# Moving the query and key projections of a pipelined self-attention ahead by one slot, placing the softmax sums between two parts of a step, and giving the last inverses a second DMA queue

## The chip, the cores and the metric

The kernel runs on one core of one Trainium2 chip. The metric is the device time of one execution in microseconds (us). Engines are named as in the profile: PE is TensorE (its weight loads are shown as PEld), DVE is VectorE, ACT is ScalarE, POOL is GpSimd, SP is SyncE, which issues the DMAs. Each engine works through its own instructions in order; what ties the engines together are waits on semaphores.

## The reference, cut to what matters

Two transformer blocks run one after the other on x of shape 8 x 512 x 256, all in float32. The first (L0) has an adaptive layer norm, self-attention with 16 heads of 16, cross-attention and a gated feed-forward. The second (L1), around which everything here turns, begins with self-attention of 16 heads of 64:

```python
q = _heads(xq @ wq)
k, v = jnp.split(ctx @ wkv, 2, axis=-1)      # here ctx is xq
q = _rope(q, sq, cq)
k = _rope(k, sk, ck)
sim = jnp.einsum('bhnd,bhmd->bhnm', q, k) * DH ** (-0.5)
a = jax.nn.softmax(sim, axis=-1)
o = jnp.einsum('bhnm,bhmd->bhnd', a, v)
o = o.transpose(0, 2, 1, 3).reshape(xq.shape[0], xq.shape[1], MID)
return o @ wo + bo
```

It is followed by a cross-attention over 64 context rows and a feed-forward with gelu.

## The kernel before, in words

The program has stages: the whole of L0 (about 24 to 880 us in the profile), the self-attention of L1 (880 to about 2057 us with its tail), the cross-attention of L1 (to about 2425 us), the feed-forward of L1 (to the end). The diff touches only the second of these, the block under the pool named "ph4". In it the order of the instructions on PE, DVE, ACT and POOL is the order in which the Python code issues them (a manual schedule over these four engines). SP is not part of it, nor are the stages that follow: their instructions are ordered by the framework's scheduler, which can also put instructions of a later stage between those of this one.

**The loop.** For each of 8 batches (`batch4`), the 16 heads are cut into 4 groups `g` of 4 heads, and the 512 keys into 4 tiles `kt`. One step `i` of the loop in `slots` stands for one pair (g, kt), 16 steps to a batch, 128 in all. Step `i` issues first `score` of its own pair, then `value` of the pair of step `i - 1`, and after every odd step the list `steps[i // 2]`, called a slot here. A group thus has four steps and two slots; slot `base + 2 * g` (with `base = 8 * b`) closes steps kt = 0 and 1 of group g, slot `base + 2 * g + 1` closes kt = 2 and 3.

- `score` (8 calls of `mm`, each two matmul instructions in the profile[...]; tile ps_S, four heads side by side) is followed by two exponentials on ACT (line 892, tile p).
- `value` has 4 calls of `mm` into the banks ps_O and ps_D, which are held for the four steps of a group. At kt = 0 POOL adds p of tile 0 and p of tile 1 (line 907, tile sm, twice); at kt = 2 DVE adds p of tiles 2 and 3 to it (line 911, four times); at kt = 3 ACT copies the two banks to oT (line 915).
- `queries(g)` and `keys(g)` both call `turned`: 4 calls of `mm` (8 instructions) into two ps_X banks, four products with the rotary tables on DVE (lines 871 and 872, tile t), a difference and a sum on POOL (lines 874 and 875, tile q or k). All matmuls have line 107, that of the helper `mm`; they are told apart by their tiles.
- `sums(g)` adds sm over the partitions with matmuls against ones, ACT copies the result (line 923, tile den), and it goes through DRAM to the layout 128 x 16: den_d is written (line 925), rec is read (line 927).
- `inverse(g)` takes the reciprocal on DVE (line 931), writes it to DRAM (line 933) and reads it back spread over the partitions, two tiles rb (line 937). `scaled(g)` multiplies the two oT of the group with them (line 942, POOL).
- `out_tiles` projects oT of all groups with w_so and adds it to x (line 396); `values` projects v (copies on line 861); `rows_` is the layer norm of the next batch (DVE statistics on lines 187, 188 and 178, POOL power on line 179, DVE result z on line 191), `turn` transposes it to hT (line 366, copies on line 367).

**Where they stand before the change.** queries(g) is in slot base + 2g - 2 and keys(g) in slot base + 2g - 1; the latter is the slot just before score(g, 0). sums(g) and inverse(g) are in slot base + 2g + 2, scaled(g) in the slot after that. The next batch's rows_, turn, queries(0) and keys(0) are in slots base - 4, base - 2, base - 2 and base - 1.

**Buffers.** ps_X has two banks, ps_S two tiles, ps_O and ps_D one each. q0, q1, k0, k1, v have two buffers, t four, p six, sm four, rb three, hT one.

**The tail.** After the last step come the values of the cross-attention to follow, `cross_values(p)` for p = 0 to 7 (2 calls of `mm`, a copy on ACT on line 830 into the two buffers named k0, and a store v_d on line 831). sums(3), inverse(3) and scaled(3) of the last batch stand before p = 2, 5 and 6. Then the last `out_tiles` follow. All these DMAs are issued by SP.

Of the kernel before, what the change touches and what calls it, by code (L numbers as in the profile page):

```python
# [17 lines left out]
B, N, D, H, T, CD, FF = 8, 512, 256, 16, 64, 192, 1024  # L18
# [60 lines left out]
def fast_path(ctx: ExitStack, tc: tile.TileContext, a: dict, out: bass.AP):  # L79

    nc = tc.nc
# [8 lines left out]
    def bank_s():  # L90
        return psum.tile([P, 2, 512], F32, tag="S", name="ps_S", bufs=2)
# [7 lines left out]
    def bank_x():  # L99
        if turns:  # L100
            turns[0] += 1
            if turns[0] % 3 == 0:
                return bank_d()
        return psum.tile([P, 512], F32, tag="X", name="ps_X", bufs=2)

    def mm(o, lhsT, rhs, start=True, stop=True):
        nc.tensor.matmul(o, lhsT, rhs, start=start, stop=stop)  # L107
# [38 lines left out]
    def check(src):  # L146
        c = checks[0]
        checks[0] += 1
        for i, op in enumerate((ALU.max, ALU.min)):
            nc.vector.tensor_reduce(chk[:, i, c : c + 1], src, AX.X, op)  # L150
# [258 lines left out]
    def flat(d):  # L409

        v = d.rearrange({2: "h n -> (h n)", 3: "j e n -> (j e n)"}[len(d.shape)])
        return v.rearrange("(p i) -> p i", p=P)
# [393 lines left out]
    def kv_first():  # L806
        w = wpool.tile([P, 2, NPAIR, 2, T], F32, tag="w4", name="kv", bufs=1)
        kvs.append((w[:, 0], w[:, 1]))
        return kvs[0]
# [6 lines left out]
    def load_vb(b):  # L816
        for e in range(2):
            r = slice(64 * e, 64 * e + 64)
            nc.sync.dma_start(kvs[b % 2][1][r, :, e, :], v_d[b, r])
# [5 lines left out]
    def cross_values(wk, p):  # L825
        ps = bank_x()
        for k in range(2):
            mm(ps, cross["v"][:, k, p * P : (p + 1) * P], ctxzT[:, k, :], k == 0, k == 1)
        v = wk.tile([P, N], F32, tag="k0", name="v")
        nc.scalar.copy(v, ps)  # L830
        nc.sync.dma_start(v_d[:, :, p, :].rearrange("b r t -> r b t"), v.rearrange("p (b t) -> p b t", b=B))


    with tc.tile_pool(name="ph4", bufs=2) as wk:
        NG = H // 4
        kb, vb = kv_first()
        steps = {}

        def last(slot, fn):
            steps.setdefault(slot, []).append(fn)  # L840

        def batch4(b):
            s = {}
            base = 2 * NG * b
# [8 lines left out]
            def values(half, ts):  # L853
                if ts[0] == 0:
                    s["v", half] = wk.tile([P, NT, 512], F32, tag="v", name="v")
                for t in ts:
                    ps = bank_x()
                    for k in range(2):
                        mm(ps, s["hT"][:, k, t * P : (t + 1) * P], w_sv[:, k, half * 512 : (half + 1) * 512],
                           k == 0, k == 1)  # L860
                    nc.scalar.copy(s["v", half][:, t, :], ps)

            def turned(g, w, tag, pss=None):

                even, odd = pss or (bank_x(), bank_x())
                for e, ps in enumerate((even, odd)):
                    for k in range(2):
                        mm(ps, w[:, k, (2 * g + e) * P : (2 * g + e + 1) * P], s["hT"][:, k, :], k == 0, k == 1)
                ec, es, oc, os = (wk.tile([P, N], F32, tag="t", name="t", bufs=4) for _ in range(4))
                for ps, c, sn in ((even, ec, es), (odd, oc, os)):  # L870
                    nc.vector.tensor_tensor(c, ps, rope_c, ALU.mult)  # L871
                    nc.vector.tensor_tensor(sn, ps, rope_s, ALU.mult)  # L872
                s[tag, g] = r = [wk.tile([P, N], F32, tag=f"{tag}{e}", name=f"{tag}{e}") for e in range(2)]
                nc.gpsimd.tensor_tensor(r[0], ec, os, ALU.subtract)  # L874
                nc.gpsimd.tensor_tensor(r[1], es, oc, ALU.add)  # L875

            def queries(g, pss=None):
                turned(g, w_sq, "q", pss)

            def keys(g, pss=None):  # L880
                turned(g, w_sk, "k", pss)
# [12 lines left out]
            def value(g, kt):  # L894
# [17 lines left out]
                if kt == NT - 1:  # L912
                    for u in range(2):
                        s["oT", 2 * g + u] = o = wk.tile([P, N], F32, tag="oT", name="oT", bufs=10)
                        nc.scalar.copy(o, s["o", u])

            def sums(g):

                d = bank_x()
                for j in range(4):  # L920
                    mm(d[32 * j : 32 * j + 32, :], ones32, s["sm", g, j // 2][:, j % 2, :])
                den = wk.tile([P, N], F32, tag="den", name="den", bufs=1)
                nc.scalar.copy(den, d)
                s["dd", g] = dd = dram.tile([4, N], F32, tag="den_d", name="den_d")
                nc.sync.dma_start(dd, den.rearrange("(j r) n -> j r n", j=4)[:, 0, :])
                s["rec", g] = rec = wk.tile([P, 4 * N // P], F32, tag="rec", name="rec")
                nc.sync.dma_start(rec, flat(dd))

            def inverse(g):
                rec = s["rec", g]  # L930
                nc.vector.reciprocal(rec, rec)
                s["inv", g] = d = dram.tile([4, N], F32, tag="rec_d", name="rec_d")
                nc.sync.dma_start(flat(d), rec)
                check(rec)
                for u in range(2):
                    s["rb", g, u] = rb = wk.tile([P, N], F32, tag="rb", name="rb", bufs=3)
                    nc.sync.dma_start(rb, d[2 * u : 2 * u + 2, None, :].to_broadcast([2, 64, N]))

            def scaled(g, engines=None):
                for u, eng in enumerate(engines or [nc.gpsimd] * 2):  # L940
# [4 lines left out]
                project_out(qp, lambda k: s["oT", k], w_so, 8, add_to(b))  # L945

            if b:
                last(base - 4, rows_)
                last(base - 2, turn)
                last(base - 2, lambda: values(0, (0, 1)))  # L950
                last(base - 2, lambda: queries(0))
                last(base - 1, lambda: values(0, (2, 3)))
                last(base - 1, lambda: keys(0))
            else:
                s["hT"] = ready

                def begin():
                    queries(0)
                    both = bank_s()
                    keys(0, (both[:, 0, :], both[:, 1, :]))  # L960
                    values(0, (0, 1))
                    values(0, (2, 3))

                last(-1, begin)
                last(4, lambda: [nc.gpsimd.memset(z, 0.0) for z in (kb, vb)])
                last(5, lambda: load_kb(0))
            for h in range(2):
                last(base + h, lambda h=h: values(1, (2 * h, 2 * h + 1)))
            for g in range(1, NG):
                last(base + 2 * g - 2, lambda g=g: queries(g))  # L970
                last(base + 2 * g - 1, lambda g=g: keys(g))
            return score, value, sums, inverse, scaled, out_tiles

        todo = [batch4(b) for b in range(B)]
        for b, (score, value, sums, inverse, scaled, out_tiles) in enumerate(todo):
            base = 2 * NG * b
            for g in range(NG):
                if b == B - 1 and g == NG - 1:
                    break
                n = base + 2 * g + 2  # L980
                steps.setdefault(n, []).insert(0, lambda g=g, f=sums: f(g))
                last(n, lambda g=g, f=inverse: f(g))
                last(n + 1, lambda g=g, f=scaled: f(g))
            if b < B - 1:
                for qp in range(2):
                    steps[base + 2 * NG + 2 + qp].insert(0, lambda qp=qp, f=out_tiles: f(qp))

        def slots():
            n = B * NG * NT
            for i in range(-2, n + 1):  # L990
                if 0 <= i < n:
                    todo[i // 16][0](i % 16 // NT, i % NT)
                if 1 <= i <= n:
                    todo[(i - 1) // 16][1]((i - 1) % 16 // NT, (i - 1) % NT)
                if i % 2:
                    for fn in steps.get(i // 2, []):
                        fn()
                if i == n - 5:
                    cross_weights()
            sums, inverse, scaled, out_tiles = todo[-1][2:6]  # L1000
            for p in range(NPAIR):
                if p == 2:
                    sums(NG - 1)
                if p == 5:
                    inverse(NG - 1)
                if p == 6:
                    scaled(NG - 1, [nc.gpsimd, nc.vector])
                cross_values(wk, p)
            load_vb(0)
            for qp in range(2):  # L1010
                out_tiles(qp)

        with tc.manual_schedule(engines={ENG.PE, ENG.DVE, ENG.Activation, ENG.Pool}):
            slots()
# [94 lines left out]
    with tc.tile_pool(name="ph6", bufs=2) as wk:  # L1109
# [22 lines left out]
        for b in range(B):  # L1132
            hT = ready
            hid = wk.tile([P, 8, N], F32, tag="hid", name="hid")
            for ff in range(4):
                ps = bank_s()
                for i in range(2):
                    f = 2 * ff + i
# [874 lines left out]
```

## Time and profile before

The time before is 2676.88 us, the median of three runs (2672.62 to 2684.0). The profiled execution has a span of 2670.4 us.

| what | us |
|---|---|
| PE busy | 2477.0 (93% of the span) |
| PE weight loads, beside the matmuls | 1170.0 |
| DVE busy | 1083.8 |
| ACT busy | 874.5 |
| POOL busy | 839.6 |
| 880 to 2015 us (self-attention of L1): PE busy of 1135.0 | 1012.84 |
| the same: DVE, ACT, POOL busy | 411.12, 347.75, 417.65 |
| one steady batch of it, 1283.73 to 1427.04: PE busy of 143.31 | 128.33 |
| 2055 to 2425 us (cross-attention of L1): PE busy of 370.0 | 347.50 |
| 2425 to 2670 us (feed-forward of L1): PE busy of 245.0 | 238.58 |

A busy time is the union of an engine's instructions. In a timeline each row gives the start, the length, the engine, the line, the operation with its tile written and tiles read, and in brackets the idle time of the engine ahead of it with the one that ended it. In the table of waits each row reads: who waited, for whom, the total in us, how often, the longest.

### The profile page before, as it was taken

How to read it: one execution, taken by the hardware profiler on the slowest of the kernel's cores; microseconds unless marked ns; L12 is line 12 of the kernel's file. 1: busy time of each engine (PE TensorE's matmuls, PEld its weight loads, DVE VectorE, ACT ScalarE, POOL GpSimd, SP SyncE). 2: the span in 40 equal slices, each digit the busy share in tenths (PEclk: the TensorE clock that was granted, in tenths of full speed). 3: DMA queues.
4: the chain of work that ended last, by engine and by line, in shares of the span. 5: the costliest groups of instructions: out<-in, count | busy, mean ns of one | idle time of the engine just before them, and what ended most of it. 6: DMA issues, size and time to landing. Idle time of an engine off the chain costs nothing.

```text
span 2670.4 us, 27976 instructions
## 1 busy us (share of the span) xinstructions
PE 2477.0 (93%) x10938; PEld 1170.0 (44%) x10938; DVE 1083.8 (41%) x2039; ACT 874.5 (33%) x1099; POOL 839.6 (31%) x521
## 2 busy tenths in 40 slices
PE   8999999999999989898998989897998999999999
PEld 3333444444355433334343434343344465556665
DVE  5554444543444243434333343334332765662100
ACT  3565554554621233232323232332321211111221
POOL 3452232233010243333333332434331534331100
PEclk9999999999999999999999999998998999999999
DMA  5120000000010000000000000000113113211000
GB/s 170 37 89 10 11 19 10 12 19 10 8 61 26 1 21 17 17 17 13 17 13 17 17 17 17 17 13 13 33 49 92 48 40 80 59 45 41 16 16 25
DMA packets 91084, 83.76 MB, mean 31 GB/s; under 512 B 51104, under 2 KB 67424, under 8 KB 90936
## 3 DMA queue, kind: packets, MB, share of 16 engines
q1 hardware_dynamic: 90944, 81.89, 10.4%
q8 instruction: 88, 1.44, 0.2%
q14 instruction: 52, 0.43, 0.1%
HBM read 72.09 MB, written 9.77 MB: 31 GB/s over the span
## 4 chain that ended last, share of the span: by engine, by line
PE 81%; DVE 8%; POOL 5%; issue 3%; DMA 2%; ACT 2%; SPq 0%; DVEq 0%; POOLq 0%; ACTq 0%
PE ps_X L107 39%; PE ps_S L107 21%; PE ps_D L107 10%; PE ps_O L107 9%; POOL k L874 1%; DVE sm L911 1%; DVE t L871 1%; POOL k L875 1%; DVE t L723 1%; DVE t L872 1%; PE ps_X L366 1%; DMA rb<-rec 1%; ACT p L505 1%; DVE st L187 1%; POOL q L724 1%
## 5 line engine op out<-in xcount | busy, mean ns | idle before, releaser
L107 PE MATMUL ps_S<-q,k 32*128 32x512 f32 (+1 forms) x3072 | 459.4, 651 | 126.5 <-POOL k L874 117.8
L892 ACT ACTIVATE p<-ps_S 128x1024 f32<-128x1024 f32 x256 | 248.1, 1021 | 649.2 <-PE ps_S L107 649.2
L107 PEld LDWEIGHTS ps_S<-q,k 32*128 32x128 f32 (+1 forms) x3072 | 173.8, 190 | 373.9 <-POOL k L874 143.5
L505 ACT ACTIVATE p<-ps_S 128x1024 f32<-128x1024 f32 x256 | 248.2, 1021 | 260.1 <-PE ps_S L107 259.1
L871 DVE TENSOR_TENSOR t<-ps_X,rope_c 128x512 f32<-128x512 f32 x126 | 86.9, 690 | 468.0 <-PE ps_X L107 468.0
L911 DVE TENSOR_TENSOR sm<-sm,p 128x1024 f32<-128x1024 f32 x128 | 184.0, 1481 | 44.8 <-ACT p L892 44.8
L907 POOL TENSOR_TENSOR sm<-p 128x1024 f32<-128x1024 f32 x64 | 149.4, 2353 | 132.3 <-ACT p L892 132.3
L396 DVE TENSOR_TENSOR x<-ps_X,x 128x512 f32<-128x512 f32 x48 | 33.2, 691 | 367.3 <-PE ps_X L107 367.3
L107 PE MATMUL ps_X<-hT,w 128*128 128x512 f32 x344 | 160.6, 601 | 1.6 <-DVE t L678 1.1
L874 POOL TENSOR_TENSOR k<-t 128x512 f32<-128x512 f32 x32 | 40.4, 1261 | 363.2 <-DVE t L872 363.2
L724 POOL TENSOR_TENSOR q<-t,t 128x512 f32<-128x512 f32 x72 | 97.3, 1354 | 157.3 <-DVE t L723 149.8
L107 PE MATMUL ps_O<-p,v 128*64 128x512 f32 x512 | 144.5, 644 | 0.0
L107 PE MATMUL ps_O<-p,h 128*32 128x512 f32 x1024 | 138.1, 612 | 0.5 <-ACT oT L518 0.5
L107 PE MATMUL ps_D<-p,v 128*64 128x512 f32 x512 | 132.7, 597 | 0.0
L107 PE MATMUL ps_X<-vw,p 128*128 128x256 f32 x512 | 120.5, 392 | 9.7 <-DVE p L1090 9.6
L179 POOL TENSOR_TENSOR rstd<-rstd,mhalf 128x4 f32<-128x4 f32 x49 | 50.7, 1035 | 244.6 <-DVE rstd L178 242.5
L107 PE MATMUL ps_X<-w_sa_wo,oT 128*128 128x256 f32 x512 | 117.9, 389 | 7.8 <-POOL oT L942 4.3
L107 PE MATMUL ps_X<-w_sa_wv,hT 128*128 128x512 f32 x256 | 118.0, 604 | 0.6
L107 PE MATMUL ps_S<-hT,w_ff_w 128*128 128x512 f32 x256 | 117.9, 604 | 0.1
L107 PE MATMUL ps_X<-hT,w_ca_wq 128*128 128x512 f32 x256 | 117.3, 598 | 0.7 <-DVE t L723 0.7
L380 POOL TENSOR_TENSOR x<-x,rows 128x1024 f32<-128x1024 f32 x24 | 56.4, 2351 | 194.2 <-DVE z L191 194.2
L107 PE MATMUL ps_X<-hT,w_sa_wq 128*128 128x512 f32 x256 | 116.0, 596 | 0.0
(219 smaller groups left out, 3539.3 us busy)
## 6 DMA issues: line engine op xcount, KB each, us to landing
rb<-rec SPq DMA_DIRECT2D x80, 256.0 KB
rb<-rec_d SPq DMA_DIRECT2D x64, 256.0 KB
x<-in_x_dram SPq DMA_DIRECT2D x8, 512.0 KB
out_dram<-x SPq DMA_DIRECT2D x8, 512.0 KB
bc<-modd SPq DMA_DIRECT2D x8, 384.0 KB
gate<-modd SPq DMA_DIRECT2D x16, 128.0 KB
k_d<-q SPq DMA_DIRECT2D x8, 256.0 KB
v_d<-v SPq DMA_DIRECT2D x8, 256.0 KB
```

What stands on the lines that cost most here:

```text
L107: nc.tensor.matmul(o, lhsT, rhs, start=start, stop=stop)
L179: nc.gpsimd.tensor_tensor(r[:, :n], r[:, :n], mhalf[:, :n], ALU.pow)
L187: nc.vector.bn_stats(st[:, t, :], src[:, t, :])
L380: nc.gpsimd.tensor_tensor(xs[b], xs[b], r[:, None, :].to_broadcast([P, NT, D]), ALU.add)
L396: nc.vector.tensor_tensor(x, ps, x, ALU.add)
L505: nc.scalar.activation(pr[u], pss[u], AF.Exp, scale=HD0 ** -0.5)
L724: nc.gpsimd.tensor_tensor(dst, t1, t2, ALU.add)
L871: nc.vector.tensor_tensor(c, ps, rope_c, ALU.mult)
L874: nc.gpsimd.tensor_tensor(r[0], ec, os, ALU.subtract)
L892: nc.scalar.activation(pr, pss[u], AF.Exp, scale=HD1 ** -0.5)
L907: nc.gpsimd.tensor_tensor(sm, s["p", g, 0, u], s["p", g, 1, u], ALU.add)
L911: nc.vector.tensor_tensor(s["sm", g, u], s["sm", g, u], s["p", g, t, u], ALU.add)
```

## The change

Three things are changed, all in the self-attention of L1 and its tail.

1. **One slot earlier.** queries(g) moves to slot base + 2g - 3, keys(g) to base + 2g - 2, and with them the next batch's rows_ (base - 5), turn and queries(0) (base - 3) and keys(0) (base - 2). values(0) stays in slots base - 2 and base - 1. The purpose is that a whole slot lies between the projection of keys and the first score that reads them.
2. **Sums between values and scores.** sums(g) no longer stands in the slot after step 4g + 5 of the batch's steps, but directly after `value` of the even step before it (dictionary `mid`), the step in which the last value product of group g is issued.
3. **The tail.** sums(3) of the last batch follows the last value product at once, before the first cross_values. Its DMAs, those of its inverse included, are issued by ACT instead of SP. They are split in two calls each (`sums_back`, `inverse_back`), placed after p = 1, 3 and 5, and scaled(3) comes after the last cross_values.

```diff
+            def queue(g):
+                return nc.scalar if (b, g) == (B - 1, NG - 1) else nc.sync
...
-                nc.sync.dma_start(dd, den.rearrange("(j r) n -> j r n", j=4)[:, 0, :])
+                queue(g).dma_start(dd, den.rearrange("(j r) n -> j r n", j=4)[:, 0, :])
...
             if b:
-                last(base - 4, rows_)
-                last(base - 2, turn)
+                last(base - 5, rows_)
+                last(base - 3, turn)
+                last(base - 3, lambda: queries(0))
                 last(base - 2, lambda: values(0, (0, 1)))
-                last(base - 2, lambda: queries(0))
+                last(base - 2, lambda: keys(0))
                 last(base - 1, lambda: values(0, (2, 3)))
-                last(base - 1, lambda: keys(0))
...
             for g in range(1, NG):
-                last(base + 2 * g - 2, lambda g=g: queries(g))
-                last(base + 2 * g - 1, lambda g=g: keys(g))
+                last(base + 2 * g - 3, lambda g=g: queries(g))
+                last(base + 2 * g - 2, lambda g=g: keys(g))
...
-                steps.setdefault(n, []).insert(0, lambda g=g, f=sums: f(g))
+                mid[n] = lambda g=g, f=sums: f(g)
...
+                if i % 2 == 0 and i // 2 in mid:
+                    mid[i // 2]()
                 if i % 2:
                     for fn in steps.get(i // 2, []):
                         fn()
...
+            sums(NG - 1)
             for p in range(NPAIR):
-                if p == 2:
-                    sums(NG - 1)
-                if p == 5:
-                    inverse(NG - 1)
-                if p == 6:
-                    scaled(NG - 1, [nc.gpsimd, nc.vector])
                 cross_values(wk, p)
+                if p % 2:
+                    (sums_back, inverse, inverse_back, lambda g: None)[p // 2](NG - 1)
+            scaled(NG - 1, [nc.gpsimd, nc.vector])
```

More of the change, by code (lines that the diff above doesn't have):

```diff
@@ L836, in fast_path @@
         kb, vb = kv_first()
-        steps = {}
+        steps, mid = {}, {}
         def last(slot, fn):
@@ L924, in sums, with sums_back @@
                 s["dd", g] = dd = dram.tile([4, N], F32, tag="den_d", name="den_d")
-                nc.sync.dma_start(dd, den.rearrange("(j r) n -> j r n", j=4)[:, 0, :])
+                queue(g).dma_start(dd, den.rearrange("(j r) n -> j r n", j=4)[:, 0, :])
+                if (b, g) != (B - 1, NG - 1):
+                    sums_back(g)
+            def sums_back(g):
                 s["rec", g] = rec = wk.tile([P, 4 * N // P], F32, tag="rec", name="rec")
-                nc.sync.dma_start(rec, flat(dd))
+                queue(g).dma_start(rec, flat(s["dd", g]))
             def inverse(g):
@@ L932, in inverse, with inverse_back @@
                 s["inv", g] = d = dram.tile([4, N], F32, tag="rec_d", name="rec_d")
-                nc.sync.dma_start(flat(d), rec)
+                queue(g).dma_start(flat(d), rec)
                 check(rec)
+                if (b, g) != (B - 1, NG - 1):
+                    inverse_back(g)
+            def inverse_back(g):
+                d = s["inv", g]
                 for u in range(2):
                     s["rb", g, u] = rb = wk.tile([P, N], F32, tag="rb", name="rb", bufs=3)
-                    nc.sync.dma_start(rb, d[2 * u : 2 * u + 2, None, :].to_broadcast([2, 64, N]))
+                    queue(g).dma_start(rb, d[2 * u : 2 * u + 2, None, :].to_broadcast([2, 64, N]))
             def scaled(g, engines=None):
@@ L969, in batch4 @@
             for g in range(1, NG):
-                last(base + 2 * g - 2, lambda g=g: queries(g))
-                last(base + 2 * g - 1, lambda g=g: keys(g))
-            return score, value, sums, inverse, scaled, out_tiles
+                last(base + 2 * g - 3, lambda g=g: queries(g))
+                last(base + 2 * g - 2, lambda g=g: keys(g))
+            tail = sums, sums_back, inverse, inverse_back, scaled, out_tiles
+            return score, value, sums, inverse, scaled, out_tiles, tail
         todo = [batch4(b) for b in range(B)]
-        for b, (score, value, sums, inverse, scaled, out_tiles) in enumerate(todo):
+        for b, (score, value, sums, inverse, scaled, out_tiles, _) in enumerate(todo):
             base = 2 * NG * b
@@ L999, in slots @@
                     cross_weights()
-            sums, inverse, scaled, out_tiles = todo[-1][2:6]
+            sums, sums_back, inverse, inverse_back, scaled, out_tiles = todo[-1][-1]
+            sums(NG - 1)
             for p in range(NPAIR):
-                if p == 2:
-                    sums(NG - 1)
-                if p == 5:
-                    inverse(NG - 1)
-                if p == 6:
-                    scaled(NG - 1, [nc.gpsimd, nc.vector])
                 cross_values(wk, p)
+                if p % 2:
+                    (sums_back, inverse, inverse_back, lambda g: None)[p // 2](NG - 1)
+            scaled(NG - 1, [nc.gpsimd, nc.vector])
             load_vb(0)
```

## The prediction

> **What bounds the kernel now.** I read the page first: its busy times, and the chain that ended last.
>
> ```profile
> span 2670.4 us, 27976 instructions
> ...
> PE 2477.0 (93%) x10938; PEld 1170.0 (44%) x10938; DVE 1083.8 (41%) x2039; ACT 874.5 (33%) x1099; POOL 839.6 (31%) x521
> ...
> PE 81%; DVE 8%; POOL 5%; issue 3%; DMA 2%; ACT 2%; SPq 0%; DVEq 0%; POOLq 0%; ACTq 0%
> ```
>
> PE is the bound, and 2670.4 - 2477.0 = 193 us of the span have no matmul. The second view is the table of waits in the stage that changes (885 to 2060 us), the rows in which PE waits or which concern the spread inverses:
>
> ```profile
> PE ps_S L107 <- POOL k L874: 117.8, 31, 13.4
> ...
> POOL oT L942 <- DMA rb<-rec_d: 42.1, 10, 16.1
> ```
>
> 31 times, once for each group but the first, the scores wait for POOL to finish the keys. That is most of the idle time of PE in the kernel. The third view is PE's timeline in one steady batch (1283.73 to 1427.04, 143.31 us): first an ordinary stall, then the one that occurs once a batch.
>
> ```profile
> 1302.14 3.60 PE L107 MATMUL ps_X<-hT,w_sa_wk 128*128 128x512 f32 x8
> 1308.60 2.36 PE L107 MATMUL ps_S<-q,k 32*128 32x512 f32 x16 [2.86 <-POOL k L874]
> ...
> 1404.38 3.70 PE L107 MATMUL ps_X<-hT,w_sa_wk 128*128 128x512 f32 x8
> 1414.04 3.80 PE L107 MATMUL ps_S<-q,k 32*128 32x512 f32 x16 [5.96 <-POOL k L874]
> 1417.77 1.98 PE L107 MATMUL ps_O<-p,v 128*64 128x512 f32 x4
> ...
> 1420.68 2.00 PE L107 MATMUL ps_S<-q,k 32*128 32x512 f32 x16
> ```
>
> The ordinary stall is pure latency: keys' matmuls, two DVE products, POOL's difference, then the scores, with nothing in between to do. The longer one comes where the next batch's layer norm holds DVE up. After it the matmuls also run slower: score plus value take 1420.68 - 1414.04 = 6.64 us, against 3.80 us elsewhere (below). The fourth view is the chain of waits in the tail:
>
> ```profile
> 2012.64 7.60 DMA v_d<-v
> ...
> 2020.98 6.93 PE ps_X L107 x8
> ...
> 2029.63 12.48 DMA rb<-rec_d
> ...
> 2042.96 13.53 PE ps_X L107 x50
> ```
>
> After the last value product (ends at 2010.0) the last projection waits for spread inverses that are issued at 2029.05 and take 12.48 us.
>
> [...]after 2.86 us of idling the scores take 2.36 us, after 5.96 us 3.80.[...]
>
> **The change part by part.**
>
> Keys a slot earlier: no operation is added, the same 8 matmuls, 4 products and 2 POOL operations move. Removed are the 31 waits, 117.8 us. For half-speed matmuls after the longer waits: the eight long ones (seven near 6, one of 13.39 us) cost 6.64 - 3.80 = 2.8 us more, 22.4 us. The 21 ordinary ones cost 4.16 - 3.80 = 0.36 us (1308.60 to 1312.76; the second half of the scores waits for POOL's second operation), 7.6 us. The two in the first batch cost 1.64 and 1.44 us. Sum 33.
>
> Is the new distance long enough? A step without extra work takes 3.80 us (1290.80 to 1294.60). After keys' last matmul the order is now step 4g - 2, step 4g - 1, then queries of the following group (3.55 us) with values (3.53), an output tile (7.01) or turn (1.52) beside it: at least 3.8 + 4.0 + 5.1 = 12.9 us. The chain needs 2.9 us when POOL is free. POOL may be in the two sums of line 907 (4.67 us), which can start once the exponentials of the step are done; keys then come about 4 us after their matmuls, 9 us ahead of need. The worst slot is now base + 3: output tile, queries, layer norm. DVE: sm until 5.5 us after the step's start, products until 16.1, statistics, power on POOL and z until 21.5. POOL: row addition until 23.9, `scaled` until 26.4, then line 907 until 31.1, then keys(3) until 33.6; their score comes at about 39.7. Thus no stall, by 6 us. Nobody waits for queries: they have another slot. The hT buffer is read by keys(3) one slot before turn overwrites it, as before.
>
> queries behind keys: they take both ps_X banks, and sums next needs one. The first is free 1.4 us after half of queries' matmuls, sums comes 3.6/2 + 3.8 us later. Hidden.
>
> sums in the even step: its 1.0 us of matmul moves. What they wait for is DVE's last addition (line 911): 5.5 us after the start of step 4g + 3 (step at 1294.60, additions end at 1300.11). PE reaches sums after that step (4.0), the slot (at least 5.1) and step 4g + 4 (3.8), 12.9 us. Behind sums on PE stand the scores; they would feel a wait, but there is none. On ACT the copy den is put ahead of the next exponentials: ACT's work in that step is 2 x 1.02 + 3 x 0.58 = 3.8 us against PE's 3.8 + 1.0, hidden. The matmuls of sums give the exponentials time: the step after one without extra work takes 4.01 to 4.07 instead of 3.80 us in the trace (it waits for ACT), so 31 x 0.25 = 7.7 us; I take 6. The reciprocal needs rec about 5.5 us after sums' start; it stands after keys' products, about 9 us after it. The products of `scaled` need rb 12.5 us after the reciprocal; in the shortest slot they come 15 us after. Both hidden.
>
> New small waits: turn is followed at once by queries, which need both halves of hT (line 367, 0.78 us each), 0.4 us x 7 = 3. Statistics of the later stages put among DVE's work near the last layer norm (they made one stall 13.39 instead of 5.96) may cost 0 to 3 again; I take 1.
>
> Tail: from the last value's end before, 46.6 us pass until the last output tile (2010.0 to 2056.6). Now: sums 1.0, copy, den_d; ACT reads rec after the second v copy, at 5.2; the reciprocal at 7.5 is off before v copies 2 and 3 have waited for their stores (2.8 to 7.6 us each); rb is issued after v copy 5, at about 13 to 17; landing 12.5 later at 26; the scaling 0.7; the first six products of the tile precede it, 11.5 us remain, 38.5 to 43. The gain is 3 to 8; I take 6.[...]
>
> Sum: 117.8 + 33 + 6 - 4 + 6 = 158.8. 2676.9 - 158.8 = 2518 us. As a check the batch: 143.31 - (2.86 + 2.85 + 2.85 + 5.96) - 3 x 0.36 - 2.84 - 0.8 = 124.1 us, while the pieces give 8 x 3.80 + 4 x 3.80 + 4 x 4.01 for steps, 8 x 3.55 for queries and keys, 4 x 3.53 for values, 4.0 for sums, 1.5 for turn, 14.0 for output: 123.6.
>
> **The rivals.**
>
> A. A new wait takes the place of the old, about the size of an ordinary stall in every group: keys behind `scaled` and line 907 on POOL, or sums behind DVE. For it: DVE's stall in the longer case, and 42.1 us of POOL waiting for rb. Against it: the margins of 6 us and more above. Then 31 x (2.5 + 0.36) = 89 us come back: 2607 us.
>
> B. The waits go, but the layer norm's slot and the tail stay bad: 7 x 3 us, and no gain in the tail (6): 2545 us. The statistics' place is not mine to see beforehand.
>
> C. Slower: each of 32 sums waits for all four of DVE's additions (5.4 us) and the half-speed matmuls follow (2.8): 32 x 8.2 = 262, giving 2780 us. For it: sums does stand in front of a score now. Against it: 12.9 us against 5.5.
>
> **How the numbers follow.** Forecast 78%, A 12%, B 7%, C 3%. The predicted time is the forecast's, 2518. Low 2500: all of 7.7 for ACT, no new waits, and 10 us more from the tail and from the stages that follow. High 2560: it takes in B and a part-way A. Faster by over 0.5% (below 2663.5): forecast, A and B, 96%; the same 1%; slower 3%.
>
> **What would show it.** The wait for POOL k gone from PE's rows or below 10 us in all; a batch of 124 to 125 us with PE idle under 2 us; scores at 2.0 and never 3.80; sums without a wait for sm; between the last value and the last output tile 38 to 43 us. The prediction is wrong if PE waits for sm, for q, or for ps_X's release by DVE, or if DVE's work of later stages lands in front of the additions.

## The result and the profile after

The changed kernel takes 2522.12 us (median of four runs, 2521.63 to 2522.75), the kernel before beside it 2674.75 us. The ratio is 0.9423, with a 95% interval of 0.94 to 0.9447. The forecast was 2518.0 us in a range of 2500 to 2560.

The page of the changed kernel answers to the one of before:

```profile
span 2520.5 us, 27970 instructions
...
PE 2437.0 (97%) x10938; PEld 1152.9 (46%) x10938; DVE 1095.1 (43%) x2039; ACT 871.3 (35%) x1099; POOL 850.9 (34%) x521
...
PE 87%; DVE 4%; DMA 3%; issue 2%; POOL 2%; ACT 2%; SPq 0%; DVEq 0%; POOLq 0%; ACTq 0%
```

PE's idle time fell from 193 to 83.5 us, and PE's busy time fell too, by 40 us, with the same 10938 matmuls: they ran less often at half speed (the mean granted clock is 0.989, 0.978 before), and the scores no longer stand open for POOL's second operation (2.00 us where those behind an ordinary stall took 2.36). In the table of waits of the stage, the row of PE waiting for POOL k is gone. These are the largest rows of PE that are left, the first two of them in the tail:

```profile
PE ps_X L107 <- DVE oT L955: 6.4, 1, 6.4
...
PE ps_X L107 <- POOL oT L955: 4.9, 1, 4.9
...
PE ps_X L107 <- ACT hT L367: 4.2, 7, 1.6
...
PE ps_X L107 <- DVE t L872: 2.4, 1, 2.4
```

PE's timeline of a steady batch shows where the scores now stand, first one right behind keys, where an ordinary stall would have been, then the one where the long stall was:

```profile
1174.00 3.60 PE L107 MATMUL ps_X<-hT,w_sa_wk 128*128 128x512 f32 x8
1177.53 2.00 PE L107 MATMUL ps_S<-q,k 32*128 32x512 f32 x16
...
1221.06 2.00 PE L107 MATMUL ps_S<-q,k 32*128 32x512 f32 x16
1222.99 1.08 PE L107 MATMUL ps_O<-p,v 128*64 128x512 f32 x4
...
1224.86 1.06 PE L107 MATMUL ps_X<-sm,ones 128*32 128x512 f32 x8
```

The score behind the keys at 1177.53 is that of the group already projected; it needs nothing from them. The one at 1221.06 is the first of group 3, the place of the 5.96 us stall. Of the 128 scores 125 take 2.00 or 2.21 us; the slowest, with 2.97 us, follows a wait in the last full batch that is shown below.

The next table is the busy time by stretch: a steady batch, then the last full one, from first output tile to first output tile. The columns are the length, then busy time and number of instructions of PE, PEld, DVE, ACT and POOL, then PE's clock, the DMA share and GB/s.

```profile
1538.17:1661.88 123.71, 123.28 (x586) 52.82 (x585) 51.60 (x75) 43.10 (x55) 53.79 (x35) 1.00 0.06 19
1661.88:1790.77 128.89, 124.97 (x585) 53.23 (x585) 66.01 (x128) 43.16 (x55) 61.00 (x41) 0.99 0.09 26
```

A steady batch takes 123.7 us instead of 143.3, with PE idle for 0.4. The last one takes 5.2 us more; DVE has 128 instructions in it, not 75. The last view is the chain in the tail:

```profile
1838.82 12.14 DMA rb<-rec_d
...
1860.41 13.57 PE ps_X L107 x32
...
1874.72 16.88 DMA rb<-rec_d
...
1892.45 13.58 PE ps_X L107 x50
```

The rb that holds the last output tiles now takes 16.88 us to land, not 12.48. I cut both spans at the last value product and at the end of the last output tile. From the stage's start (878.1 before, 877.8 after) to the last value product (2010.1, 1859.2) it is 1132.0 us before and 981.4 after, 150.6 less. From there to the last output tile (2056.5, 1906.0) it is 46.4 and 46.8. The rest takes 613.9 and 614.5. So the whole gain lies in the loop, and the tail as a whole gave nothing.

### The profile page after: what moved, and what is told of

Read it like the earlier page. It is cut to its first block, busy times and chain, and to the rows that moved or that the text cites. A ratio compares the mean times of both kernels' runs of the same rounds, so it can differ in the third digit from the quotient of the medians.

```text
span 2520.5 us, 27970 instructions
## 1 busy us (share of the span) xinstructions
PE 2437.0 (97%) x10938; PEld 1152.9 (46%) x10938; DVE 1095.1 (43%) x2039; ACT 871.3 (35%) x1099; POOL 850.9 (34%) x521
## 4 chain that ended last, share of the span: by engine, by line
PE 87%; DVE 4%; DMA 3%; issue 2%; POOL 2%; ACT 2%; SPq 0%; DVEq 0%; POOLq 0%; ACTq 0%
PE ps_X L107 42%; PE ps_S L107 22%; PE ps_D L107 11%; PE ps_O L107 9%; PE ps_X L366 1%; DMA rb<-rec_d 1%; DVE t L723 1%; ACT p L505 1%; POOL q L724 1%; DMA rb<-rec 1%; DVE t L720 1%; DVE st L187 1%; PE ps_X L485 0%; POOL p L1104 0%; PE ps_X L527 0%
## 5 line engine op out<-in xcount | busy, mean ns | idle before, releaser
L107 PE MATMUL ps_S<-q,k 32*128 32x512 f32 (+1 forms) x3072 | 432.5, 628 | 7.0 <-ACT p L505 3.4
L107 PEld LDWEIGHTS ps_S<-q,k 32*128 32x128 f32 (+1 forms) x3072 | 160.6, 185 | 245.7 <-issue 136.4
L911 DVE TENSOR_TENSOR sm<-sm,p 128x1024 f32<-128x1024 f32 x128 | 192.3, 1546 | 55.6 <-ACT p L892 54.3
L874 POOL TENSOR_TENSOR q<-t 128x512 f32<-128x512 f32 x32 | 40.7, 1273 | 384.2 <-DVE t L872 384.2
L107 PE MATMUL ps_O<-p,v 128*64 128x512 f32 x512 | 138.0, 617 | 0.0
```

Of the source, the lines that this page charges most:

```text
L911: nc.vector.tensor_tensor(s["sm", g, u], s["sm", g, u], s["p", g, t, u], ALU.add)
```

## The experiments

### Each part alone

**Queries and keys ahead, alone.** The two pairs of lines of the first part, applied to the kernel before:

```diff
-                last(base + 2 * g - 2, lambda g=g: queries(g))
-                last(base + 2 * g - 1, lambda g=g: keys(g))
+                last(base + 2 * g - 3, lambda g=g: queries(g))
+                last(base + 2 * g - 2, lambda g=g: keys(g))
```

(and the same shift for the next batch's norm, turn, queries and keys).

> Only the first part of the change: queries, keys and the next batch's norm and turn one slot earlier; sums and the tail as before. Theory L (the gain is latency of the projection, taken off PE's path by a slot of distance): the 31 waits for POOL k (117.8 us) and the half-speed matmuls (33 us) go, small new waits of 3 us and late statistics of 5 us come, so 2532 us, and the row of PE waiting for POOL k is gone. Theory S (the sums have to leave the slot as well, because there they stand on PE before the projection): half of the stalls stay, 2590 us.

2522.57 us, ratio 0.9433 (0.9414 to 0.9452). That is the time of the whole change, better than theory L had it; theory S falls. The stretches of this kernel, a steady batch and the last full one, show what the other parts do:

```profile
1047.31:1172.11 124.80, 124.37 (x589) 54.95 (x585) 51.36 (x75) 43.37 (x54) 53.82 (x35) 1.00 0.05 18
1671.29:1796.94 125.65, 124.36 (x588) 54.95 (x584) 66.03 (x128) 43.37 (x54) 61.05 (x41) 1.00 0.08 26
```

A steady batch is 1.1 us longer than in the changed kernel, so moving the sums is worth 1.1 us a batch there. But the last batch loses only 0.85 us to the same 53 extra DVE instructions that cost the changed kernel 5.2.

**Sums between values and scores, alone.**

```diff
-                steps.setdefault(n, []).insert(0, lambda g=g, f=sums: f(g))
+                mid[n] = lambda g=g, f=sums: f(g)
...
+                if i % 2 == 0 and i // 2 in mid:
+                    mid[i // 2]()
```

> Only the second part: sums directly after the last value products of a group; projections and tail as before. Theory L: PE still waits 2.85 us for each keys; only the exponentials' wait of 0.25 us per group goes, 2667 to 2675 us. Theory S: the sums were what held the chain, 2640 us or less.

2679.54 us against 2672.98, ratio 1.0021 (1.0012 to 1.0031): a little slower, outside both theories' numbers. PE waits for POOL k 31 times as before, 118.3 us. The timeline of PE shows what is new, an ordinary stall of 2.86 us after which the score takes 3.80 us, as long as behind a long stall (over 1170 to 1600 us the mean granted clock is 0.96 here and 0.98 in the kernel before):

```profile
1379.78 3.60 PE L107 MATMUL ps_X<-hT,w_sa_wk 128*128 128x512 f32 x8
1386.24 3.80 PE L107 MATMUL ps_S<-q,k 32*128 32x512 f32 x16 [2.86 <-POOL k L874]
```

In the kernel before, the ordinary stalls of steady batches were followed by a score of 2.36 us. Here several take between 3.2 and 3.8 us. The 0.25 us per group that ACT gives back is more than used up by that.

**The tail alone.** The third part of the diff, applied to the kernel before.

> Only the third part: sums(3) of the last batch at once, its DMAs from ACT, split and spread between the cross_values. By the prediction's step 6 us are gained: 2669 us. By the trace of the changed kernel (46.9 us from the last value product to the last output tile against 46.6 before) nothing is: 2675 us, within 5.

2676.33 us, ratio 1.0009 (0.9995 to 1.0022). No gain in the time.

**The changed kernel without its tail part.**

> The changed kernel without its third part. By the prediction's step 6 us are lost: 2528 us. If the queue of its own gains nothing, 2522 us within 3; if it costs (the last spread inverse took 16.88 us to land, against 12.48 before), 2517 us.

2519.82 us (2515.24 to 2524.46), ratio to before 0.9425 (0.9401 to 0.945). Against the changed kernel's 0.9423 this is no difference that can be told from the times. The traces, one execution each, tell more. From the last value product to the last output tile it is 43.2 us here and 46.8 in the changed kernel; with the old loop it is 46.4 without the third part and 49.8 with it. So in both pairs the third part makes this stretch about 3.5 us longer. The last spread inverse shows where, issued by SP in this run and by ACT in the run of the tail alone:

```profile
1876.05 12.23 DMA rb<-rec_d
...
2034.37 16.95 DMA rb<-rec_d
```

In the kernel before it is 12.48 us from SP, in the changed kernel 16.88 from ACT. Why the read takes longer on the second queue is not shown.

### What has to stand between a projection and its score

**Keys first, queries last.** The kernel before with queries and keys exchanged.

```diff
-                last(base + 2 * g - 2, lambda g=g: queries(g))
-                last(base + 2 * g - 1, lambda g=g: keys(g))
+                last(base + 2 * g - 2, lambda g=g: keys(g))
+                last(base + 2 * g - 1, lambda g=g: queries(g))
```

> The kernel before with the two projections of a group exchanged: keys(g) in slot base + 2g - 2, queries(g) in base + 2g - 1, for every group but the first batch's first. Theory L (whatever is projected in the last slot before a score stalls it, by the latency of its own chain): 2673 us within 10, PE now waits for POOL q, 31 times, 2.85 us and more each. Theory K (it is keys that stall, because their POOL operations stand behind others or because their tile is the stationary one): most of 150 us is gained, 2540 us.

2672.06 us, ratio 0.9999 (0.9985 to 1.0013). The table of waits has the same stalls under another name:

```profile
PE ps_S L107 <- POOL q L874: 117.5, 31, 13.4
```

117.5 us for 117.8. Keys are not special. The projection that comes last before the score stalls it, whichever it is.

**Only the layer norm earlier.** The kernel before with one line changed.

```diff
-                last(base - 4, rows_)
+                last(base - 5, rows_)
```

> The kernel before with only the next batch's layer norm one slot earlier (base - 5 for base - 4), everything else as it was. By the prediction's split the long stall of a batch (5.96 us and 2.84 us of half-speed matmuls) becomes an ordinary one (2.85 and 0.36): 7 x 5.6 = 39 us less, 2634 us. Rival (the norm's DVE work only stalls another group instead): 2673 us, with the long stall at another score of the batch.

2648.78 us, ratio 0.9916 (0.9899 to 0.9933): 24 us of the 39. The waits went as forecast; the longest stall is now 3.1 us:

```profile
PE ps_S L107 <- POOL k L874: 88.9, 31, 3.1
```

117.8 - 88.9 = 28.9 us of waits are gone, and by the split the end of the long stalls' half-speed matmuls should have added 17. It did not, since now many ordinary stalls are followed by scores of up to 3.80 us, as in the run with the sums alone (the last section has the clock over this one, 0.50):

```profile
1335.65 3.80 PE L107 MATMUL ps_S<-q,k 32*128 32x512 f32 x16 [2.85 <-POOL k L874]
```

Of the 31 scores behind a stall, 19 take 2.8 us or more here.

**Keys late, queries of the next group behind them.** The changed kernel with keys(g) back in the slot before its score. There the queries of the following group come after them.

```diff
-                last(base + 2 * g - 2, lambda g=g: keys(g))
+                last(base + 2 * g - 1, lambda g=g: keys(g))
```

(and keys(0) of the next batch at base - 1; the list of a slot is made with setdefault where the output tiles go into it.)

> The changed kernel with keys(g) moved back into the slot just before their score (base + 2g - 1), where the queries of the following group now stand behind them. Theory L (only the latency has to be covered: 2.86 us, and the 3.6 us of these queries' matmuls do it): 2525 us within 8, no wait for POOL k of more than 10 us in all. Rival (a slot of distance is needed, since POOL and DVE have other work in front): 2580 us or more.

2556.83 us, ratio 0.9574 (0.9558 to 0.959), between the two theories. The stalls of the scores are indeed gone: one wait for POOL k, 2.8 us. In the ordinary groups 3.6 us of other matmuls are enough cover. What is new stands at the turn:

```profile
PE ps_X L366 <- DVE t L872: 20.9, 7, 7.0
```

Here is that place in one batch, across the engines:

```profile
1218.55 4.67 POOL L907 TENSOR_TENSOR sm<-p 128x1024 f32<-128x1024 f32 x2
...
1220.93 6.78 DVE L911 TENSOR_TENSOR sm<-sm,p 128x1024 f32<-128x1024 f32 x4 [5.09 <-POOL sm L907]
...
1222.91 3.70 PE L107 MATMUL ps_X<-hT,w_sa_wk 128*128 128x512 f32 x8
...
1227.63 0.68 DVE L871 TENSOR_TENSOR t<-ps_X,rope_c 128x512 f32<-128x512 f32 x1
...
1228.96 0.82 PE L366 MATMUL ps_X<-ident,z 128*128 128x128 f32 x4 [2.34 <-DVE t L872]
...
1231.56 5.88 PE L107 MATMUL ps_X<-hT,w_sa_wq 128*128 128x512 f32 x8
```

With the slot before it empty of projections, the steps reach this slot before POOL has caught up with norm and scaling. Its two sums end late, DVE's additions follow, and the products that release the two ps_X banks stand behind them in DVE's order. The transposes need those banks; the queries after them take 5.88 us instead of 3.6. A batch takes 129.3 us (from the output tile at 1048.30 to that at 1177.64). So it is the latency that must be covered, but here the slot of distance also keeps the slots evenly filled and the banks free when the next user comes.

### The batch that is 5 us longer

**One buffer for the statistics.** The changed kernel with one buffer instead of four for the layer norm's statistics:

```diff
-        st = small.tile([P, NT, 6], F32, tag="st", name="st")
-        mv = small.tile([P, NT, 2], F32, tag="mv", name="mv")
+        st = small.tile([P, NT, 6], F32, tag="st", name="st", bufs=1)
+        mv = small.tile([P, NT, 2], F32, tag="mv", name="mv", bufs=1)
```

> The changed kernel with one buffer instead of four for the two tiles of layer norm statistics (st and mv), so that fewer statistics of the later stages can be put among DVE's work in the last batch. Theory H (these statistics, some 15 us of DVE in the slots after 1692 us, are why that batch takes 128.89 instead of 123.70 us): 5 us less, 2517 us, if the later stages don't mind. Rival: the later stages lose as much by the missing buffers, 2522 us or more.

2532.48 us, ratio 0.9473 (0.9457 to 0.9489), slower than the changed kernel. The last full batch is cured, with 101 DVE instructions where there were 128:

```profile
1661.59:1785.83 124.24, 123.35 (x587) 52.83 (x585) 61.48 (x101) 43.16 (x55) 58.12 (x38) 1.00 0.09 27
```

124.24 us for 128.89. But from the last output tile on (1899.6 to 2529.8) it takes 630.2 us, 15.7 more than the 614.5 of the changed kernel. Theory H is right on the cause and the rival on the sum: the later stages need those buffers.

### The tail: two DMA engines or the queue

**The spread inverses in halves.** An rb has 128 partitions, read from two rows of DRAM. The edit, in the changed kernel:

```diff
-                    queue(g).dma_start(rb, d[2 * u : 2 * u + 2, None, :].to_broadcast([2, 64, N]))
+                    for j in range(2):
+                        queue(g).dma_start(rb[64 * j : 64 * j + 64, :], d[2 * u + j, None, :].to_broadcast([64, N]))
```

> The changed kernel with each spread inverse rb read in two DMAs, one for each half of the partitions[...]. Theory E (an rb takes 12 to 17 us because it runs on two DMA engines): it lands within 5 us, the last output tiles lose their waits of 4.88 and 6.36 us, and the last group's 4 us of stalls shrink: 2508 us. Theory Q (it takes that long because it stands behind the stores v_d and the weight loads on shared engines): 2522 us.

2503.61 us, ratio to before 0.9363 (0.9347 to 0.9379), so 18.5 us below the changed kernel. In the timeline of the tail the four reads are issued, and both products of `scaled` and the output tiles come at once:

```profile
1872.91 2.44 ACTq L951 DMA_DIRECT2D rb<-rec_d  x4
...
1877.34 1.27 POOL L956 TENSOR_TENSOR oT<-oT,rb 128x512 f32<-128x512 f32 x1 [17.28 <-DMA rb<-rec_d]
1878.29 0.87 DVE L956 TENSOR_TENSOR oT<-oT,rb 128x512 f32<-128x512 f32 x1 [10.04 <-DMA rb<-rec_d]
```

The last product starts 5.4 us after the first issue, although the same stores v_d are under way. The output tiles run in one piece of 14.17 us. From the last value product (1859.2) to their end (1890.3) it is 31.0 us, not 46.8. Theory E holds; the next run's trace has the share of the DMA engines beside it.

**The halves alone, on the kernel before.**

> The kernel before with the spread inverses read in halves[...], nothing else. If the two DMA engines held up the tail before as well: its waits of 4.34 and 3.47 us and some of the half-speed matmuls after them go, 2660 us. If only the tail as the change has it profits: 2673 us.

2655.3 us, ratio 0.9944 (0.9931 to 0.9956): 17.6 us less, as much as on the changed kernel and more than expected. The tail's end moves by 16 us. The slow read was there before the change, and the two gains add up. These are two stretches in which the spread inverses are nearly all that is under way, in the kernel before and in this one; the last three columns are PE's clock, the DMA share and GB/s:

```profile
2034.00:2039.00 5.00, 0.73 (x2) 0.50 (x2) 0.00 (x0) 0.00 (x0) 1.26 (x1) 0.87 0.13 50
...
2025.00:2027.00 2.00, 2.00 (x11) 1.75 (x10) 0.00 (x0) 0.59 (x1) 0.00 (x0) 1.00 0.60 197
```

A share of 0.13 of 16 engines is as much as 2.1 busy engines, 0.60 as much as 9.6, and the rate is four times as high. That also rules out that the gain comes merely from having four reads in place of two with as few engines busy.

**The halves without the queue of its own.**

> The changed kernel with the inverses in halves and without its third part: the tail in its old order, all its DMAs from SP. If the queue of its own is worth something once an rb is quick: 2509 us, behind the 2503.6 of the kernel in halves with the third part. If it is not: 2502 us.

2507.22 us, ratio 0.9387 (0.9371 to 0.9404), against 0.9363 (0.9347 to 0.9379) with the third part. The intervals overlap; the medians differ by 3.6 us in favour of the third part, but the traces do not bear it out (30.0 us from the last value product to the last output tile here, 31.0 with the third part), so this isn't settled.

**The halves, with the last sums behind the first cross_values.**

```diff
-            sums(NG - 1)
             for p in range(NPAIR):
                 cross_values(wk, p)
+                if p == 0:
+                    sums(NG - 1)
```

> The changed kernel in halves, and the last sums after the first cross_values instead of before it, so that PE doesn't wait for the last addition of sm (0.98 us[...]): 2501.5 us, 2 us less than in halves alone. Rival: the den chain, 1.7 us later, then ends the tail, 2504 us.

2502.28 us, ratio 0.936 (0.9345 to 0.9376). It is the fastest of all these kernels, but its lead of 1.3 us on the halves alone is less than their runs differ.

## Why the prediction was right, point by point

**The waits for keys (117.8 us).** Right, and shown. They go with the first part alone, and with the exchange of queries and keys they stay, at 117.5 us. It is latency on PE's path, and the projection that comes last sets it.

**The half-speed matmuls (33 us).** That they ran at half speed is shown: behind the long stall in the prediction's timeline the granted clock is 0.50 from 1413.09 to 1419.92. Close as a sum, with a miscount in it: to the last value product the loop lost 150.6 us where the waits, these matmuls, ACT's relief and the small waits had been put at 117.8 + 33 + 6 - 4 = 152.8. The working counts eight long stalls and 21 ordinary ones; the trace of the kernel before has seven long ones (six near 6 us, one of 13.39) and 22 ordinary ones, which makes the term 30.6. That 150.4 would then meet 150.6 is partly luck, since the sums gave less than their 6 us (below). The 0.36 us of an ordinary stall were not half speed either: the granted clock over such a score is 1.00, and the delay is POOL's second operation (the weight loads of the scores wait for it 31 times, 26.5 us in all). Nor did every stall of that length leave the clock at 1.00: the two scores behind stalls of 2.79 and 2.85 us in the first batch took 3.37 and 3.45 us, at a mean clock of 0.57.

The split into 2.8 us for a long stall and 0.36 for an ordinary one holds only for the order of the kernel before. In two runs that leave the stalls but shift them, ordinary ones cost up to 3.0 us as well. So removing all stalls pays more surely than removing some.

**The margins.** Right in the steady batches: no wait of a score, 123.7 us for a forecast of 124.1, turn's wait for hT 4.2 us in all for a forecast of 3. The run with keys late shows that the margins were not idle: with one slot less, the ps_X banks are released too late at the turn.

**The sums (6 us).** The size per batch was right, 1.1 us (124.80 against 123.70), over seven batches 7.7. But only 3.8 us of it are left at the end of the loop (967.9 us from its first score to the last value product with the first part alone, 964.1 in the changed kernel), and little of it reaches the total (2519.82 us with the first two parts, 2522.57 with the first alone, intervals that overlap), and this the prediction did not have: the last full batch gives 4.3 us back beyond what it loses without this part (128.89 against 125.65, where a steady batch is 1.1 us shorter). There DVE works late on statistics of later stages, and sums, standing earlier on PE, wait 2.35 us for a ps_X bank that DVE has yet to release:

```profile
1723.22 1.73 PE L107 MATMUL ps_X<-sm,ones 128*32 128x512 f32 x8 [2.35 <-DVE t L872]
```

The term "0 to 3 again; I take 1" for these statistics was too small: 5.2 us in this batch.

**The tail (6 us).** Wrong: it gained nothing, by 46.4 against 46.8 us, and in the traces of the two runs that leave it out or take it alone it cost about 3.5 us. Three steps of its sum failed. "Sums 1.0" ended 4.3 us after the last value product, because the scaling of group 1 on POOL waited for its own slow rb until 1851.09, its sums and then DVE's additions came late, and sums waited 1.22 us for them and took 3.06 us, not 1.06, at a mean clock of 0.51.

"Landing 12.5 later" became 16.88: that a second queue would help was the author's estimate, and by the runs it goes with the longer landing. And "11.5 us remain" were 13.6, because after the wait the last output tiles ran at a granted clock of 0.50 up to 1897.57; the kernel before has 13.53 there, at a mean clock of 0.81, so this was to be seen. The issue itself was where the working had it, 14.9 us after the last value product for 13 to 17. The 12.48 us are also not the time of one read alone: two reads of 256 KB are issued 0.6 us apart (from 2029.05), the first is in use at 2036.95, and up to there (from 2033.50) all that was under way took a DMA share of 0.13 and moved 50 GB/s. That these reads stood in the prediction's sum as given, and were not taken as the lever, is the oversight: the run in halves shows 18.5 us there.

**The sum.** 158.8 us were forecast; the medians differ by 152.6, the spans of the two profiled executions by 149.9. By the spans, the loop to the last value product is 2.2 us short (150.6 for 152.8), the tail 6.4 (a loss of 0.4 for a gain of 6), the later stages 0.6, and the stage's start gives 0.3 back. That the time came within 4.1 us owes something to the base: the forecast subtracts from 2676.88 us, while the medians of the kernel before beside the experiments are 2672.6 to 2673.0, so that the gain was overestimated by some 8 us.

**The rivals.** A, a new wait of the old size in each group, did not occur; it does when keys are moved back, but once a batch and on a ps_X bank. B came true in its second half: a bad batch and a tail without gain, at a smaller size. C did not occur. Of the prediction's own signs of being wrong three showed, each in one place: PE waited 1.22 us for sm in the tail and 2.35 us for a ps_X bank, and statistics of later stages stood in front of DVE's additions in the last full batch. In the steady batches none did.

## What to carry to other kernels

When a strict order of instructions lets an engine wait for the last link of a short chain on other engines, look at which link comes last before the consumer, and put matmuls of another unit of work between them: here 2.86 us of latency and more, 31 times, were nearly 6% of the kernel together with the clock that fell (to 0.50 behind the long ones). Check for each slot who releases the buffers that the moved work needs, since an emptied or a doubled slot moves the wait to a bank. And try a slow broadcast DMA in more pieces: four reads of 64 partitions each were in use 5.4 us after the first issue where two of 2 x 64 took 13 to 18.

## What the runs showed of the hardware that was not expected

A stall of PE of the same length, 2.85 us, is followed by a score of 2.36 us in one order of the work and of 3.80 us in another, as the runs with sums alone and with the norm earlier show. The granted clock differs with it. Here are two stretches around a stall in the kernel before (1305.74 to 1308.60), then two around one of the run with the norm earlier (1332.80 to 1335.65). The columns are the stretch, its length, PE's busy time and number of instructions, the clock, the DMA share and GB/s:

```profile
1303.86:1307.28 3.42, 1.88 (x5) 1.00 0.08 33
1307.28:1310.69 3.41, 2.01 (x16) 1.00 0.00 0
...
1331.63:1335.05 3.42, 1.17 (x3) 1.00 0.06 24
1335.05:1338.46 3.41, 2.81 (x16) 0.50 0.02 5
```

Around the first stall the clock stays at 1.00; around the second it is 1.00 up to 1335.05, 0.60 us before the stall's end, and 0.50 in the stretch from there. The length of a stall does not tell them apart: in the run with the norm earlier the 19 slow scores stand behind stalls of 2.79 to 2.86 us, while two stalls of 3.14 and 3.15 us are followed by scores of 2.36 us. In the kernel before, the half clock of the long stalls begins every 143.36 us from 983.01 to 1699.81, where a batch takes 143.31, and after its first batch all its ordinary stalls are followed by scores of 2.36 us. The edits that shift the stalls without removing them lost that. What decides whether the clock falls behind a stall is not shown. A row's time after a stall is thus no fixed price.
